# Link counts of a graph network layer: source nodes in rows and a fixed span of destination columns, and a fourth buffer of gathered rows

## Chip, cores and metric

The kernel runs on one core of one Trainium2 chip. The metric is device time in microseconds (us), the median of repeated runs. The core has a matrix engine (PE; PEld is its loading of weights), a vector engine (DVE), an activation engine (ACT), GpSimd (POOL), a queue engine (SP) and 16 DMA engines. On-chip memory is SBUF; matmul results land in PSUM, in banks of 512 f32 per partition.

## What is computed

There are 1250 nodes with 512 features (384 "vector", 128 "scalar") and 40000 edges, sorted by destination. The layer is PaiNN-like, followed by a residual and a layernorm:

```python
s_j = silu(x[src][:, 384:] @ W1 + b1) @ W3 + b3
edge_basis = rbf(edge_weight) * cutoff @ W2 + b2
s1, s2, s3 = thirds(s_j * edge_basis)
msg = concat(v_j * s1 + s3 * edge_attr, s2)          # first sums: over edges
x = x + segment_sum(msg, dst)
# node update: v@U, v@V, norm, an MLP, three factors -> row(x), a function of the node alone
x = x + segment_sum(row(x)[src], dst)                # second sums
out = layernorm(x0 + x)
```

The second sums need no edges once the number of links from each source node to each destination node is known: they are a matrix of link counts (dst x src) times the matrix of rows. The kernel makes these counts while it makes the first sums.

## The kernel before, in words

**Front.** Edges are cut into 79 chunks of 512 and laid out in rows. DVE tests that every edge lies in a window, and `by_tile` turns each field (source, destination less the chunk's first destination, weight, three attributes) with PE transposes into tiles of 128 edges. Then a table of node rows (640 wide) is made and written to DRAM.

**The loop over edge batches.** Four chunks make a group (20 groups, `g`). A step `t` of the loop takes four tiles of 128 edges, one of each chunk; a group has four steps, so there are 80 steps. In a step:

- POOL issues four indirect DMAs (`gather`, L649) that fetch 128 table rows each into `rows_t`, which has three buffers; the gather for step t+2 is issued in step t.
- PE makes the edge factors `eb` of the next step (`edge_factors`, L745). `eb` has one buffer, so this waits until DVE has finished the messages of the present step.
- DVE makes the messages (`messages`, L757 and L758) from `rows_t` and `eb`, then a one-hot of the source node's low part (`mark_sources`, L772), 256 wide.
- PE sums the messages of the step before (`add_messages`, L787 and L794) into `agg`, and counts its links (`count_links`, L811) into `adj`. Here the stationary operand is the hat function `pair` (32 columns for the 32 destination nodes of a chunk's window, one set for each of `PARTS` = 4 parts of the sources); the one-hot is the moving operand. Four tiles sit side by side in the array, each in 32 columns, so 16 matmuls of 256 columns a step.
- ACT makes the hats of the next group in `make_pair` (four L732, 128 wide, and one L737, 512 wide, a step).

1280 padded nodes don't fit into 4 x 256 sources; the fifth part is counted with a weight of 2^-11 on top of the first and split off later by DVE (`split_first`, L834 and L836).

**Closing a group.** After the group's last step, ACT copies `agg` and three quarters of `adj` out of PSUM (`close_group`, L821, L825, L826), DVE does `split_first`, and `hand_over` sends the rows that belong to a neighbouring block of nodes to `beside_s` and `beside_l` by DMAs on SP.

**A block of 128 nodes** (10 blocks, one for each two groups) is updated in ten steps that are spread through the loop: `make_sel` (DVE, then an ACT copy, L869) builds the selection of rows, `sum_block` (PE, L878) brings the first sums into node order, `take_block` adds them, `turn_nodes`, `times_u`, `u_times`, `times_v`, `lengths`, `hidden`, `factors`, `end_row` are small PE and ACT work through one PSUM buffer `work`, and `scale_row` (DVE, L1006 and L1012) needs the factor `s1` that ACT copies in L1000. `count_block` (L905, with an ACT copy L914) brings the counts of the block into node order: 30 matmuls for each block, in three of its steps.

**The second sums** (`add_out`, L1080) are 300 matmuls of 512 columns with `counts` as weights; most of them are spread over the last ten steps, after the last gather.

What sets the order: the program is recorded by hand. In each step the queues are filled in this order: gather, messages, mark_sources, the list `first`, add_messages and count_links of the step before, the list `early` (close_group, make_pair, block updates), edge_factors of the next step, the list `late`, the list `dve`. Every engine works through its own queue in that order.

```python
at(early, last_step[g] + 1, close_group, g)
at(early, t, make_pair, g + 1, i)
begin = max(last_step[last_source(b)] + 1, begin + 5)
at(dve, begin, make_sel, b)
at(late, begin + 4, count_block, b, BANK // P)
at(early, begin + 8, factors, b)
at(dve, begin + 8, scale_row, b)
```

The sine's arguments `turn` lie in the memory of `counts` until the first counts are written; most of their products are made on ACT in the first steps (`start_sine`, L671), 20 instructions.

Of the kernel before, what the change touches and what calls it, by code (L numbers as in the profile page):

```python
# [38 lines left out]
PARTS = 4  # L39
FIFTH = 2.0**-11  # L40
# [17 lines left out]
def gnn_resnorm(  # L58
# [121 lines left out]
    diff = const.tile([P, P], I32)  # L180
# [16 lines left out]
    sh.diff, sh.ident, sh.lane, sh.part, sh.half_n = diff, ident, lane, part, half_n  # L197
# [13 lines left out]
    nc.vector.tensor_scalar(share, part[:NCP, :], float(per_chunk), None, op0=ALU.mult)  # L211
# [4 lines left out]
    for values, bound, op in (  # L216
        (local_r, 0.0, ALU.is_lt),
        (away_r, float(-MARGIN), ALU.is_lt),
        (away_r, float(per_chunk + MARGIN - 1), ALU.is_gt),
    ):  # L220
        nc.vector.scalar_tensor_tensor(off, values, bound, off, op0=op, op1=ALU.max)
# [13 lines left out]
    sh.local = fields.tile([P, NGR, TPC * CPG], F32, name="local")  # L235
    sh.weight = fields.tile([P, NGR, TPC * CPG], F32, name="weight")
# [7 lines left out]
    with tc.tile_pool(name="ps_front", bufs=3, space=PSUM) as ps_front:  # L244
# [18 lines left out]
        for k in range(3):  # L263
            by_tile(att_r, k, 3, sh.attr[:, :, :, k])

# [213 lines left out]
def windowed(tc, sh):  # L479
# [18 lines left out]
    assert NP <= (PARTS + 1) * LOW and P == 2 * GSPAN and MARGIN <= GSPAN // CPG  # L498
# [43 lines left out]
    counts = keep.tile([P, NB, NB, P], F16, name="counts")  # L542
# [9 lines left out]
    with tc.tile_pool(name="msg", bufs=4) as pool, tc.tile_pool(  # L552
# [11 lines left out]
        turn = counts.rearrange("s b a n -> s (b a n)").bitcast(F32)[:, : NGR * N_RBF * EPG]  # L564
        turn = turn.rearrange("p (g n t) -> p g n t", n=N_RBF, t=EPG)
# [9 lines left out]
        column = pool.tile([P, NE], F32, name="column", bufs=1)  # L575
        fifth_e = pool.tile([P, NE], F32, name="fifth_e", bufs=1)
# [15 lines left out]
        def split_sources(half):  # L592
            if half == 0:
                nc.vector.tensor_scalar(fifth_e, src_f, PARTS * LOW - 0.5, None, op0=ALU.is_gt)
                nc.vector.scalar_tensor_tensor(
                    column, fifth_e, -float(PARTS * LOW), src_f, op0=ALU.mult, op1=ALU.add
                )
                nc.vector.tensor_scalar(
                    part, column, 1.0 / LOW, -0.5 + 0.5 / LOW, op0=ALU.mult, op1=ALU.add
# [5 lines left out]
                column[:, :, None].to_broadcast([P, NE, 2]), op0=ALU.mult, op1=ALU.add,  # L605
            )
            nc.vector.scalar_tensor_tensor(
                column, part, -float(WIN), sh.local.rearrange("p g t -> p (g t)"),
                op0=ALU.mult, op1=ALU.subtract,
            )  # L610
            nc.vector.tensor_scalar(fifth_e, fifth_e, 1.0 - FIFTH, None, op0=ALU.mult)
            nc.vector.scalar_tensor_tensor(
                column, column, 4.0, fifth_e, op0=ALU.mult, op1=ALU.add
# [4 lines left out]
        place = pool.tile([P, NB, 3, 2], F16, name="place", bufs=1)  # L618
        beside_s = pool.tile([P, 2, width], F32, name="beside_s", bufs=1)
        beside_l = pool.tile([P, 2, NP], F16, name="beside_l", bufs=1)  # L620
        nc.gpsimd.memset(beside_s, 0.0)
        nc.gpsimd.memset(beside_l, 0.0)
        def find_places():
            nc.vector.memset(place, -1.0)
            for b in range(NB):
                def put(rows, slot, g):
                    nc.vector.tensor_scalar(
                        place[rows, b, slot, :], sh.node[rows, g : g + 1].to_broadcast([rows.stop - rows.start, 2]),
                        float(-b * P), None, op0=ALU.add,
# [12 lines left out]
        aggs, adjs, sums, links, ebs, pairs, both_of = {}, {}, {}, {}, {}, {}, {}  # L642

        def gather(t):
            g, i = batches[t]
            rows_t = pool.tile([P, CPG, V + 2 * C], F32, name="rows_t", bufs=3)
# [13 lines left out]
        def start_turns(g, n):  # L660
# [4 lines left out]
                turn[:, g : g + n], share[:, :, None, :].to_broadcast(shape),  # L665
                sh.half_n[:, None, :, None].to_broadcast(shape),
            )

        def start_sine(g, k):

# [130 lines left out]
        def count_links(t):  # L801
            g, i = batches[t]
            if i == 0:
                adjs[g] = ps_sum.tile([P, PARTS * LOW], F32, name="adj")
# [768 lines left out]
```

## Time and profile before

| what | value |
|---|---|
| median of 14 runs | 612.78 us (610.52 to 618.65) |
| the profiled execution's own time | 612.09 us |
| its span | 610.3 us |
| mean granted clock of PE in the span | 0.908 |
| PE busy | 510.5 us, 84% |
| DVE busy | 443.8 us, 73% |
| POOL busy | 341.9 us, 56% |
| ACT busy | 302.2 us, 50% |
| first gather starts, last gather ends | 72.55 us, 493.56 us |

Reading it: busy shares are averages over stages with different limits. The front runs to about 72 us, the loop over gathered edges from there to about 500 us, the second sums and the layernorm to the end. Times in a view count from the start of the span. "Idle before, releaser" is how long the engine sat idle before an instruction and what ended that. The granted clock is a share of full speed. Matmul durations overlap, so for PE the chain of waits, or starts, tell more than the mean of one.

### The profile page before, as it was taken

Reading aid. Unit: us, or ns where it says so; the run is one execution under the profiler, and the core shown is the slowest. Engines: PE = TensorE matmul, PEld = TensorE weight load, DVE = VectorE, ACT = ScalarE, POOL = GpSimd, SP = SyncE. Lnnn points to the kernel's source line nnn. Section 1 sums busy time; section 2 is a strip of 40 time slices with the busy share of each in tenths; the row PEclk is TensorE's granted clock in tenths of the full one; section 3 lists DMA queues with packets and bytes.
Section 4 is the critical chain, followed back from the end, with each engine's and each line's share of the span. In section 5 each row is a group of like instructions: output and inputs, shape, how many; then the busy total and the mean of one; then the engine's idle time right before and its main releaser. Section 6 shows DMA issues by size and latency. Waiting matters only on the chain.

```text
span 610.3 us, 13655 instructions
## 1 busy us (share of the span) xinstructions
PE 510.5 (84%) x5626; PEld 280.4 (46%) x5626; DVE 443.8 (73%) x606; ACT 302.2 (50%) x717; POOL 341.9 (56%) x343
## 2 busy tenths in 40 slices
PE   1578547676999998998999998998888999999993
PEld 1322223233455455555554564564554645555441
DVE  4334069899789889999988898899989863020583
ACT  1210547255367468575684585675774632323200
POOL 2200177677777777777877777777777720044000
PEclk9965568799789889999998898899999899999997
DMA  8112288788978988888889888888788730701021
GB/s 242 49 64 86 91 253 259 224 246 250 286 241 252 288 253 257 267 254 271 249 252 283 253 259 266 256 257 264 229 269 262 241 106 18 261 27 72 35 86 53
DMA packets 37229, 124.12 MB, mean 203 GB/s; under 512 B 6738, under 2 KB 8104, under 8 KB 37158
## 3 DMA queue, kind: packets, MB, share of 16 engines
q0 software_dynamic: 25008, 102.42, 55.3%
q1 hardware_dynamic: 8230, 13.00, 6.1%
q10 hardware_dynamic: 3920, 7.74, 3.7%
q8 instruction: 46, 0.75, 0.5%
q14 instruction: 25, 0.20, 0.1%
HBM read 112.02 MB, written 8.46 MB: 197 GB/s over the span
## 4 chain that ended last, share of the span: by engine, by line
PE 50%; DMA 12%; DVE 11%; POOL 10%; issue 9%; ACT 8%; SPq 1%; DVEq 0%; POOLq 0%; ACTq 0%
POOL rows_t L649 10%; DMA rows_t<-table,src_i 9%; PE agg L787 7%; PE work L878 5%; PE eb L745 5%; PE agg L794 5%; PE adj L1080 4%; PE eb L1080 4%; DVE msg L758 3%; PE work L905 3%; PE adj L811 3%; ACT pair L732 2%; DVE msg L757 2%; PE agg L1080 2%; PE work L970 2%
## 5 line engine op out<-in xcount | busy, mean ns | idle before, releaser
L649 POOL DMA_INDIRECT rows_t<-table,src_i x313 | 320.7, 1025 | 150.1 <-issue 81.3
L758 DVE TENSOR_TENSOR msg<-rows_t,eb 128x1536 f32<-128x1536 f32 (+1 forms) x81 | 137.0, 1692 | 0.0
L757 DVE TENSOR_TENSOR msg<-rows_t,eb 128x1024 f32<-128x1024 f32 (+1 forms) x81 | 95.6, 1180 | 48.6 <-PE eb L745 23.4
L745 PE MATMUL eb<-w_sb,basis_t 21*128 21x384 f32 x626 | 78.5, 551 | 43.5 <-DVE msg L758 42.7
L732 ACT ACTIVATE pair<-number,column 128x128 f16<-128x128 f16 x320 | 102.0, 394 | 0.0
L787 PE MATMUL agg<-msg,hot 128*32 128x512 f32 x626 | 93.8, 656 | 0.0
L794 PEld LDWEIGHTS agg<-msg,spread 128*32 128x32 f32 x1878 | 58.9, 116 | 55.8 <-issue 55.5
L794 PE MATMUL agg<-msg,spread 128*32 128x128 f32 x1878 | 71.5, 282 | 0.0
L745 PEld LDWEIGHTS eb<-w_sb,basis_t 21*128 21x128 f32 x626 | 27.7, 189 | 62.3 <-issue 49.2
L811 PE MATMUL adj<-one,pair 128*32 128x256 f16 x1252 | 51.5, 276 | 4.0 <-DVE link L836 4.0
L772 DVE TENSOR_TENSOR one<-number,low 128x1024 f16<-128x1024 f16 (+1 forms) x81 | 53.8, 665 | 0.0
L737 ACT ACTIVATE pair<-pair 128x512 f16<-128x512 f16 x80 | 50.4, 630 | 2.5
L1080 PEld LDWEIGHTS <-counts 128*128 128x128 f16 x300 | 29.2, 98 | 33.0 <-issue 1.4
L1072 POOL TENSOR_TENSOR msg<-msg,rows_t 128x512 f32<-128x512 f32 (+1 forms) x10 | 13.0, 1328 | 52.4 <-PE work L990 41.9
L811 PEld LDWEIGHTS <-pair 128*32 128x32 f16 x1252 | 36.1, 98 | 5.7 <-issue 4.5
L720 DVE TENSOR_TENSOR spread<-hot,attr 128x768 f32<-128x768 f32 x40 | 38.0, 951 | 0.0
L905 PE MATMUL work<-sel_s,link 128*128 128x128 f16 x200 | 21.8, 230 | 12.1 <-ACT vu L939 11.4
L914 ACT ACTIVATE counts<-work 128x512 f16<-128x512 f32 (+1 forms) x30 | 15.8, 526 | 31.5 <-PE work L905 31.5
L1080 PE MATMUL eb<-store,counts 128*128 128x512 bf16 x120 | 28.5, 379 | 0.0
L703 ACT COPY basis_t<-work 128x512 f32<-128x512 f32 x20 | 11.7, 585 | 33.7 <-PE work L698 33.7
L905 PEld LDWEIGHTS <-link 128*128 128x128 f16 x200 | 16.2, 102 | 26.3 <-issue 25.3
L1027 ACT CAST store<-x 128x512 bf16<-128x512 f32 x10 | 6.2, 617 | 44.0 <-DVE x L1026 44.0
(177 smaller groups left out, 665.2 us busy)
## 6 DMA issues: line engine op xcount, KB each, us to landing
rows_t<-table,src_i POOLq DMA_INDIRECT x313
table<-msg SPq DMA_DIRECT2D x10, 320.0 KB
resid<-x SPq DMA_DIRECT2D x10, 256.0 KB
msg<-resid ACTq DMA_DIRECT2D x2, 1280.0 KB
out_dram<-msg SPq DMA_DIRECT2D x9, 256.0 KB
store<-in_x_dram ACTq DMA_DIRECT2D x2, 1024.0 KB
beside_l<-link SPq DMA_DIRECT2D x18, 80.0 KB
rows_t<-in_x_dram ACTq DMA_DIRECT2D x1, 1280.0 KB
```

The source lines that it names most:

```text
L649: nc.gpsimd.indirect_dma_start(out=rows_t[:n, j, :], out_offset=None, in_=sh.table1, in_offset=bass.IndirectOffsetOnAxis(ap=sh.src_i[:n, g ...
L732: nc.scalar.activation(pair[:, e, :], number[:, : PARTS * WIN], AF.Abs, scale=4.0, bias=column[:, g * EPG + e : g * EPG + e + 1],)
L737: nc.scalar.activation(quarter, quarter, AF.Relu, scale=-1.0, bias=1.0)
L745: nc.tensor.matmul(eb[:, j, :V], turned[g][rows, i, :], sh.w2_sb[rows, :], start=True, stop=True,)
L757: nc.vector.tensor_mul(msg[:m, js, V:], rows_t[:m, js, V:], eb[:m, js, C:V])
L758: nc.vector.tensor_mul(msg[:m, js, :V].rearrange("p t (k c) -> p t k c", k=3), rows_t[:m, js, :V].rearrange("p t (k c) -> p t k c", k=3), ...
L772: nc.vector.tensor_tensor(one[:m, js, :].rearrange("p t (l h) -> p t l h", h=2), number[:m, :].rearrange("p (l h) -> p l h", h=2)[:, None] ...
L787: nc.tensor.matmul(agg[j * WIN : (j + 1) * WIN, :], hots[g][:m, i * CPG + j, :], msg[:m, j, :width], start=(i == 0), stop=False, skip_grou ...
L794: nc.tensor.matmul(agg[j * WIN : (j + 1) * WIN, c * C : (c + 1) * C], spread[g][:m, i * CPG + j, c, :], msg[:m, j, width:], start=False, s ...
L811: nc.tensor.matmul(adj[j * WIN : (j + 1) * WIN, k * LOW : (k + 1) * LOW], pairs[g][:m, i * CPG + j, k * WIN : (k + 1) * WIN], one[:m, j, : ...
L905: nc.tensor.matmul(out[:, a * P : (a + 1) * P], t[:rows, (first + a) * P : (first + a + 1) * P], sels[b][1][:rows, n, :], start=(k == 0), ...
L1080: nc.tensor.matmul(acc, counts[:, b, a, :], table2(a, k), start=(a == 0 and k == 0), stop=(a == NB - 1 and k == 2),)
```

## The change

The counts are now summed with the *source* nodes in the rows. `count_links` takes the one-hot as stationary operand, in two halves of 128 source nodes, and the hats as moving operand: for each tile and each half one matmul, 128 rows out, 5 x 48 = 240 columns. The 48 columns are a fixed span of destination nodes, the same for all edges of a chunk (16 of the chunk's own and a margin of 16 on each side), and no longer the 32 from the chunk's first destination; `PARTS` is 5, so the weight of 2^-11 and `split_first` go. A group covers 96 columns, of which 32 overlap with the group before: `close_group` copies the new 64 for all parts into `counts` (ACT, 640 elements), and `add_counts` adds the overlapping 32 to what stands there (DVE, 320 elements). `counts` is then in the order in which `add_out` uses it: `count_block`, the `link` tiles, `beside_l` with its DMAs and the small selection are gone; the big selection is made by DVE directly. `make_pair` is 240 wide (and 960 for its second pass). A field `away` is turned in the front in addition. `turn` gets a small tile of its own for two groups and its products are made in `make_turns` on DVE; `start_turns` and `start_sine` go. `rows_t` gets a fourth buffer; the gather for step t+2 is still issued in step t. `beside_s` with two slots becomes `flank` with one.

```diff
-PARTS = 4
-FIFTH = 2.0**-11
+PARTS = 5
+SPAN = GSPAN // CPG + 2 * MARGIN
+REACH = GSPAN - GSPAN // CPG + SPAN
...
+        by_tile(away_r, 0, 1, sh.away)
...
-    counts = keep.tile([P, NB, NB, P], F16, name="counts")
+    counts = keep.tile([P, NB, NGR * GSPAN + REACH], F16, name="counts")
+    by_group = counts.rearrange("s (p h) n -> s h p n", h=2)
...
-            rows_t = pool.tile([P, CPG, V + 2 * C], F32, name="rows_t", bufs=3)
+            rows_t = pool.tile([P, CPG, V + 2 * C], F32, name="rows_t", bufs=4)
...
-        def start_turns(g, n):
+        def make_turns(g, n):
...
-                turn[:, g : g + n], share[:, :, None, :].to_broadcast(shape),
+                turn[:, :n], share[:, :, None, :].to_broadcast(shape),
...
-                pairs[g] = pool.tile([P, EPG, PARTS * WIN], F16, name="pair", bufs=2)
+                pairs[g] = pool.tile([P, EPG, PARTS * SPAN], F16, name="pair", bufs=2)
...
-                    pair[:, e, :], number[:, : PARTS * WIN], AF.Abs, scale=4.0,
+                    pair[:, e, :], number[:, : PARTS * SPAN], AF.Abs,
...
-                adjs[g] = ps_sum.tile([P, PARTS * LOW], F32, name="adj")
+                adjs[g] = ps_sum.tile([P, 2, BANK], F32, name="adj")
...
-            for k in range(PARTS):
+            for h in range(2):
+                to = adj[:, h, : PARTS * REACH].rearrange("s (p n) -> s p n", n=REACH)
...
+                    at = j * (GSPAN // CPG)
...
-                        adj[j * WIN : (j + 1) * WIN, k * LOW : (k + 1) * LOW],
-                        pairs[g][:m, i * CPG + j, k * WIN : (k + 1) * WIN], one[:m, j, :],
+                        to[:, :, at : at + SPAN], one[:m, j, h * P : (h + 1) * P],
+                        pairs[g][:m, i * CPG + j, :].rearrange("e (p n) -> e p n", n=SPAN),
...
-            nc.scalar.copy(link[:rows, LOW:BANK], adj[:rows, LOW:BANK])
-            nc.scalar.copy(link[:rows, BANK : PARTS * LOW], adj[:rows, BANK:])
...
-        def split_first(g):
...
+            adj = adjs[g][:, :, : PARTS * REACH].rearrange("s h (p n) -> s h p n", n=REACH)
+            new, reach = REACH - GSPAN if g else 0, tiles(g, 0)[-1] * GSPAN // CPG + SPAN
+            nc.scalar.copy(
+                by_group[:, :, :, g * GSPAN + new : g * GSPAN + reach], adj[:, :, :, new:reach]
+            )
+
+        def add_counts(g):
+            adj = adjs.pop(g)[:, :, : PARTS * REACH].rearrange("s h (p n) -> s h p n", n=REACH)
+            if g:
+                to = by_group[:, :, :, g * GSPAN : (g + 1) * GSPAN - (2 * GSPAN - REACH)]
+                nc.vector.tensor_add(to, to, adj[:, :, :, : REACH - GSPAN])
...
-            nc.sync.dma_start(beside_s[rows, slot, :], sums[g][rows, :])
-            nc.sync.dma_start(beside_l[rows, slot, :], links[g][rows, :])
+            nc.sync.dma_start(flank[rows, :], sums[g][rows, :])
...
-            sel = pool.tile([P, 3, P], F32, name="sel", bufs=1)
-            nc.scalar.copy(sel, small)
-            sels[b] = sel, small
+            sels[b] = sel
...
-        def count_block(b, first):
...
-                        acc, counts[:, b, a, :], table2(a, k),
+                        acc, counts[:, a, MARGIN + b * P : MARGIN + (b + 1) * P], table2(a, k),
...
-        at(dve, 0, start_turns, 1, 2)
-        for k in range(N_RBF):
-            at(late, 1 + k * 4 // N_RBF, start_sine, 3, k)
...
-            at(dve, last_step[g] + 1, split_first, g)
+            at(dve, last_step[g] + 1, add_counts, g)
...
-            at(late, begin + 3, count_block, b, 0)
...
-            at(late, begin + 4, count_block, b, BANK // P)
...
-            at(late, begin + 5, count_block, b, 2 * BANK // P)
```

## The prediction

> **What bounds the kernel now.** I read the page's busy shares first, then the table of stretches by block of nodes, then the chain of waits for the tail, then the timeline of single steps.
>
> ```profile
> PE 510.5 (84%) x5626; PEld 280.4 (46%) x5626; DVE 443.8 (73%) x606; ACT 302.2 (50%) x717; POOL 341.9 (56%) x343
> L649 POOL DMA_INDIRECT rows_t<-table,src_i x313 | 320.7, 1025 | 150.1 <-issue 81.3
> ...
> 115.49 1.15 POOL L649 DMA_INDIRECT rows_t<-table,src_i  x1 [2.25 <-DVE msg L758]
> ```
>
> POOL's 56% hides a full queue. From 72.55 to 493.56 us it gathers, and each of 313 gathers costs its 1.025 us plus about 0.30 us of issue: 1.325 us, so 32 gathers (one block of nodes, eight steps) can't take less than 42.4 us. In all that time it waited only some 5 us for a buffer, 2.25 of them at 115.49.
>
> ```profile
> core 0: us, PE busy (x) PEld busy (x) DVE busy (x) ACT busy (x) POOL busy (x), PEclk, DMA share, GB/s
> 156.90:200.80 43.90, 40.52 (x535) 23.52 (x534) 38.37 (x44) 27.02 (x65) 33.85 (x34) 0.93 0.84 259
> 244.10:285.00 40.90, 37.59 (x535) 22.37 (x536) 39.48 (x46) 27.89 (x67) 31.46 (x32) 1.00 0.86 261
> 370.60:414.90 44.30, 40.90 (x535) 23.57 (x536) 39.56 (x46) 28.22 (x68) 33.88 (x34) 0.92 0.85 260
> ```
>
> These are three of the seven blocks between 156.9 and 456.9 (300.0 us, 42.86 us each). DVE works 39.5 us in the block of 40.9 us: there DVE is the bound, with 1.4 us of waits. In the blocks of about 44 us the granted clock is 0.92 to 0.93. So three limits lie within 3 us of each other: POOL 42.4, DVE 40.9 (with its waits), and PE when its clock drops.
>
> ```profile
> 384.00:388.00 4.00, 2.77 (x50) 1.85 (x43) 3.96 (x7) 3.36 (x9) 3.09 (x4) 1.00 0.81 247
> 388.00:392.00 4.00, 3.80 (x40) 2.23 (x43) 3.97 (x6) 2.54 (x7) 3.08 (x4) 0.57 0.78 240
> ...
> 388.20 0.27 PE L905 MATMUL work<-sel_s,link 128*128 128x128 f16 x2 [1.40 <-ACT vu L939]
> 389.25 1.94 PE L787 MATMUL agg<-msg,hot 128*32 128x512 f32 x8
> ```
>
> PE stood 1.40 us at the second `count_block` of the block, because `work` has one buffer and ACT's copy (L939) stands behind `make_pair`; then the clock was 0.57 and `add_messages` took twice its time. Five blocks have this; their step starts of L757 are 6.4 to 7.1 us apart, where undisturbed ones are 4.7.
>
> ```profile
> 409.21 0.25 ACT L1000 COPY s<-work 128x128 f32<-128x128 f32 x1
> 409.49 0.56 DVE L1006 TENSOR_TENSOR x<-vu,s 128x384 f32<-128x384 f32 x1 [0.57 <-ACT s L1000]
> ...
> 496.68 1.70 PE adj L811 x12
> 511.99 0.83 PE work L905 x12
> 516.33 0.83 PE work L905 x12
> 520.39 0.34 PE work L905 x6
> 538.05 0.69 PE work L905 x12
> ```
>
> The first pair shows DVE waiting on ACT once in every block. The others are pieces of the chain that ended last: after about 463 us it is nearly all PE, so there each PE instruction less is time less.
>
> **The change, part by part.** The sum is made against the profiled execution: 612.09 us, of which 610.3 are the span. It lies 0.7 us under the median of 612.78, well within the runs' spread.
>
> *Front, +0.7.* `by_tile(away)` puts four transposes behind the twelve of the attributes; four cost 0.74 us (L253, local_r). PE, the test, DVE's first work and the table's chain follow one another there, so I take it whole; ends 0 and +1.2 (with ACT's 0.43 copy). Shorter `split_sources` and one memset instead of two (L621 0.96, L622 2.24) lie beside the table's chain, which waits on PE and ACT: nothing.
>
> *Fourth buffer, -2.0.* The wait at 115.49 goes (2.25 less the usual 0.30). What is late next is DVE: the step that starts at 101.43 takes it 10.9 us (`find_places` 5.6) and now loses L834 and L836 (0.84), since `add_counts` does nothing for group 0; with those the 4.0 us that PE waited for L836 once go too. Ends -2.0 and 0. Later waits for a buffer are 0.05 to 0.3 us each: nothing.
>
> *PE in a step.* Now 16 matmuls in 0.44 us (chain, L811 at full clock). After: 8 of 240 columns. L905 starts 128 columns every 0.056 us, L1080 512 columns every 0.215, both with full 128x128 weights; between them 240 columns cost 0.10, so 0.82: +0.38 a step, 3.0 a block (ends 0.45 and 1.72 for the eight, by the two rows). Gone are 30 matmuls a block (0.78, 0.78 and 0.44 us) and the stall of 1.2 to 1.4: -3.3. PE's sum stays, but it is laid out evenly.
>
> *ACT in a step.* L732 (128 wide) follow each other by 0.295, L737 (512 wide) takes 0.63; slope 0.61 to 0.86 ns an element (the second from L821 against L1000). So 4 x 0.07 to 0.10 and 0.27 to 0.39: +0.55 to +0.77 a step. Gone are L914, L825, L826, L869 and L671; the new copy of 640 elements costs about 0.70 (L821's slope). ACT's total has room (28 of 42 us), its order has not: the root in `lengths` stands behind `make_pair`, `hidden` and `add_messages` behind it on PE, then ACT's two copies, `make_pair` again, and only then `s1`. That is +0.55 (first pass), +0.38 (longer counts), +0.55 (second pass), less 0.15 (copies): `s1` comes 1.3 us later, ends 0.8 and 2.1. DVE stands in `scale_row` for it; behind it are `make_sel` and the next messages, and PE's next `eb` waits for these.
>
> *DVE in a block.* Minus 0.83 twice (L834, L836); plus 0.49 twice (`add_counts`, 320 elements on L836's 0.42 for 256); plus 0.82 (L664's product, now every second group); plus 0.15 (f32 selection). Of the savings, those just before the wait for `s1` are lost in it.
>
> *A block's period.* 40.9 (undisturbed) - 0.4 + 0.82 + 0.15 + 1.3 + 0.3 (two steps where PE is now level with DVE) = 43.1. Half-clock spells at L905 go with their stall; those at `sum_block` (L878 4.46 against 2.77 us, about every second block, after a wait for DVE that stays) leave 0.2: 43.3 against 42.86, seven times: +3.1. Ends: POOL's floor of 42.4 gives -3.2; `s1` 2.1 late and spells in every block, 44.5, gives +11.
>
> [...]
>
> *Last block of the loop (456.9 to 501.3), -2.0.* Its stall and spell go (1.5); the mixed step, where 12 matmuls over tiles of 128 and 64 rows took 1.70, becomes six of 0.10 (-1.1); some 0.6 is given back as above. Ends -5 and +1.
>
> *Tail, -5.1.* Before 517.15 the L905 at 511.99 and 516.33 go, and ACT's copies in between shrink; PE is then ready for L1080 at about 514.1, when ACT's last copy lands: -3.05. Behind that PE is full, so L905's 0.34, 0.69, 0.69 and 0.34 are all time: -2.06. Ends -6.5 and -3.
>
> *Free.* [...] The DVE product may hold a gather up (the one beside L664 took 1.40 instead of 0.95): at most 4.5 us over ten blocks, covered by the 0.9 us a block between POOL's floor and 43.3, and paid if DVE were quicker.
>
> Sum: 0.7 - 2.0 + 3.1 - 2.0 - 5.1 = -5.3: 606.8 us.
>
> **The rivals.**
>
> *`s1` decides (slower).* ACT's longer passes make DVE wait in each block. For it: L1006 already waits for L1000 in most blocks. Against it: ACT idles a third of a block. It turns the sign when the block exceeds 44.05 us, which is `s1` 2.1 late; at 2.6 late, 44.6: +12.2 instead of +3.1, 615.9 us.
>
> *POOL becomes the clean bound (much faster).* With the stall gone PE keeps full clock, the fourth buffer takes up every unevenness, and a block costs 42.4: 606.8 - 6.3 = 600.5 us. For it: the three blocks at clock 1.00 need 40.9 to 42.2. Against: `s1`.
>
> *Full-width counting costs PE what L1080 costs.* If strided sums of 5 x 48 columns cost 0.215 each, a step gains 1.3 us of PE, a block 7 more: about 45.5, +18: 622 us. Nothing in the trace speaks for it but the missing row.
>
> *No gain in the tail.* If the last counts hold L1080 up by 3 us, the tail saves 2.1 and the time is about 610.
>
> **How the numbers follow.** Forecast as summed (604 to 609.5) 0.38; POOL's floor 0.22; nothing much (609.7 to 615.8) 0.20; `s1` 0.14; PE 0.06. Half a per cent, 3.1 us, is about what a measurement of this kernel can tell. Under 609.7: 0.38 + 0.22 = 0.60, less 0.02 for the forecast's upper edge, 0.58; over 615.8: `s1` and PE, 0.20; between: 0.20 + 0.02 = 0.22. The ends of all terms reach 595 and 622; 8 in 10 lie in 598.5 to 616; the likeliest case alone lies in 603 to 611.
>
> **What the profile after would show.** Eight matmuls of 240 columns a step in 0.8 us; no wait of 1.4 us and no drop of clock in the block's fifth step; DVE's wait for `s1` about 2.2 us a block; ACT's passes 0.36 and 0.9 us; POOL without the 2.25; L1080 starting about 6 us earlier than 517. Wrong if DVE's wait for `s1` is under 1 us or over 3, if the eight matmuls cost over 1.1 us, or if half-clock spells are as many as before.

## The result, and the profile after

The changed kernel takes 635.3 us (median, 631.3 to 637.8), the kernel before 613.0: a ratio of 1.036 (95% interval 1.033 to 1.039). It is slower by 22 us where 6 us less were forecast, and it lies far above the range. Lines of `kernel.py` have moved: the messages are L741 and L742 (before L757, L758), `count_links` L797 (L811), `edge_factors` L729 (L745), `sum_block` L852 (L878), the copy of `s1` L954 (L1000), `add_out` L1034 (L1080), the gather L643 (L649).

The page of after: busy shares, and the granted clock in 40 slices of the span (the second fence is before's row of the same view).

```profile
PE 528.1 (84%) x4704; PEld 288.2 (46%) x4704; DVE 442.5 (70%) x590; ACT 333.5 (53%) x638; POOL 343.4 (55%) x342
PEclk9965579889997987987987987987987999999998
```

```profile
PEclk9965568799789889999998898899999899999997
```

PE has 922 matmuls fewer and is busy 18 us longer. From the thirteenth slice to the thirty-first, that is from about 190 to 490 us, its clock falls to 0.7 in every third slice. The table of stretches shows the loop (columns: stretch, length, busy time of PE, weight loads, DVE, ACT and POOL, granted clock, share and rate of the DMAs):

```profile
core 0: us, PE busy (x) PEld busy (x) DVE busy (x) ACT busy (x) POOL busy (x), PEclk, DMA share, GB/s
244.00:292.00 48.00, 43.36 (x441) 24.58 (x441) 40.38 (x45) 31.67 (x60) 35.84 (x35) 0.89 0.81 249
387.00:435.00 48.00, 43.29 (x441) 24.64 (x440) 40.02 (x45) 31.67 (x60) 33.67 (x33) 0.89 0.76 229
```

A block of eight steps takes 47.65 us on average from step 21 to step 69, and 47.8 in each of the last three of these; before it took 42.65 between the same steps. No engine is full in it: PE works 43.3 us of 48, DVE 40, POOL 33.5. Cut at the starts of the messages of steps 0, 21, 69 and 79 and at the first matmul of the second sums, the spans compare so (us; the last column is an experiment told below):

| stretch | before | after | filler_long |
|---|---|---|---|
| front, to step 0 | 81.1 | 78.4 | 77.7 |
| steps 0 to 21 | 115.0 | 113.2 | 114.1 |
| steps 21 to 69, six blocks | 255.9 | 285.9 | 260.1 |
| steps 69 to 79 | 49.3 | 50.2 | 47.1 |
| step 79 to the first matmul of the second sums | 15.7 | 11.0 | 10.9 |
| from there to the end | 93.3 | 91.2 | 91.3 |
| span | 610.3 | 629.9 | 601.2 |

Up to step 21 the changed kernel is 4.5 us ahead, and it saves 6.8 us behind step 79. The six blocks between lose 30.0. This is one of them on PE (the timeline of after: start, us, operation, count, and in brackets how long PE had been idle and what ended it):

```profile
317.92 0.93 PE L729 MATMUL eb<-w_sb,basis_t 21*128 21x384 f32 x8 [1.34 <-DVE msg L742]
319.13 0.65 PE L682 MATMUL work<-ident,basis 128*128 128x128 f32 x4 [0.28 <-ACT vv L916]
319.71 1.86 PE L771 MATMUL agg<-msg,hot 128*32 128x512 f32 x8
321.32 1.53 PE L778 MATMUL agg<-msg,spread 128*32 128x128 f32 x24
326.47 1.07 PE L771 MATMUL agg<-msg,hot 128*32 128x512 f32 x8
...
337.18 1.66 PE L729 MATMUL eb<-w_sb,basis_t 21*128 21x384 f32 x8 [2.07 <-DVE msg L742]
338.77 3.78 PE L852 MATMUL work<-sums,sel 128*128 128x512 f32 x4
```

The same eight `add_messages` take 1.86 us at 319.71 and 1.07 at 326.47. PE idles 1.34 and 0.28 us, works at half clock for 3.4 us, idles 2.07 us some steps later, and works at half clock for 6.8. On DVE (timeline of after) the first idle place begins with the product (L658, 0.82 us), the second with the wait for `s1`; each spell comes back as a wait for `eb`:

```profile
312.77 0.82 DVE L658 TENSOR_TENSOR turn<-weight,half_n 128x640 f32<-128x640 f32 x1
325.97 1.22 DVE L741 TENSOR_TENSOR msg<-rows_t,eb 128x1024 f32<-128x1024 f32 x1 [2.12 <-PE eb L729]
332.62 0.56 DVE L960 TENSOR_TENSOR x<-vu,s 128x384 f32<-128x384 f32 x1 [1.90 <-ACT s L954]
338.90 1.22 DVE L741 TENSOR_TENSOR msg<-rows_t,eb 128x1024 f32<-128x1024 f32 x1 [1.27 <-PE eb L729]
347.57 1.22 DVE L741 TENSOR_TENSOR msg<-rows_t,eb 128x1024 f32<-128x1024 f32 x1 [1.96 <-PE eb L729]
```

Where do the spells begin and end? In steps of 0.25 us, the granted clock of after falls at 289.1, 319.9, 336.9, 367.6, 384.7 us: 9 and 5 times 3.413 us apart, in turn. The shorter of the spells, from 319.85 to 323.26, lasts 3.41 us itself, and from the fall at 108.23 to that at 480.28 it is 109 times 3.413. So I cut the loop into stretches of 3.413 us that end where a spell begins (the table of stretches again):

```profile
313.02:316.43 3.41, 3.41 (x50) 2.30 (x46) 3.34 (x5) 1.83 (x6) 2.55 (x3) 1.00 0.90 260
316.43:319.85 3.42, 1.79 (x18) 0.90 (x20) 3.42 (x5) 2.64 (x7) 2.75 (x3) 1.00 0.78 262
319.85:323.26 3.41, 3.41 (x35) 1.69 (x31) 3.41 (x4) 3.36 (x7) 2.50 (x4) 0.50 0.83 226
323.26:326.67 3.41, 3.41 (x29) 2.55 (x31) 1.29 (x2) 2.59 (x3) 2.80 (x3) 1.00 0.78 246
333.50:336.91 3.41, 1.42 (x8) 0.98 (x6) 3.41 (x4) 3.35 (x8) 1.44 (x2) 1.00 0.85 236
336.91:340.33 3.42, 3.15 (x10) 1.38 (x11) 2.15 (x4) 1.71 (x3) 2.42 (x3) 0.50 0.45 137
340.33:343.74 3.41, 3.41 (x5) 1.01 (x3) 3.25 (x4) 0.00 (x0) 2.80 (x3) 0.50 0.84 237
343.74:347.15 3.41, 3.41 (x49) 1.87 (x48) 1.50 (x3) 0.62 (x1) 2.50 (x4) 1.00 0.87 236
```

All 28 changes of the clock of after between 120 and 530 us lie at edges of this grid. PE was busy for 0.52 and 0.42 of the stretches ahead of the spells. In after, of 98 stretches at full clock between 120 and 530 us, the 13 in which PE was busy for less than 0.55 are all followed by half clock, and of the 85 at 0.63 and above one is (0.69). In after, half clock ended only behind a stretch that was full, and the second spell, which began with 0.3 us of idle time, lasted twice as long; in three_buffers_2 and more_work it also ended behind 0.95 and 0.96, so that this is no exact rule.

The trace of before has a grid of the same step: its clock falls at 327.1, 344.2, 371.5 and 388.6 us, 5, 8 and 5 times 3.413 us apart. Nine of its ten spells between 120 and 530 us follow stretches with shares of 0.39 to 0.61, though between 0.52 and 0.61 eight were followed by half clock and seven were not. The tenth, at 501.22, follows a stretch in which the profile has PE busy throughout (1.00, in 19 matmuls). So the share goes with the spells, but it is not what the clock goes by.

### The profile page after: what moved, and what is told of

Same layout as the page of the kernel before. It is cut to its first block, busy times and chain, and to the rows that moved or that the text cites. A ratio compares the mean times of both kernels' runs of the same rounds, so it can differ in the third digit from the quotient of the medians.

```text
span 629.9 us, 11657 instructions
## 1 busy us (share of the span) xinstructions
PE 528.1 (84%) x4704; PEld 288.2 (46%) x4704; DVE 442.5 (70%) x590; ACT 333.5 (53%) x638; POOL 343.4 (55%) x342
## 4 chain that ended last, share of the span: by engine, by line
PE 32%; DVE 20%; POOL 18%; DMA 13%; issue 12%; ACT 3%; DVEq 0%; SPq 0%; POOLq 0%; ACTq 0%
POOL rows_t L643 18%; DMA rows_t<-table,src_i 11%; DVE msg L742 7%; PE work L852 5%; DVE msg L741 4%; PE adj L1034 4%; PE eb L1034 4%; PE eb L729 3%; PE agg L771 2%; DVE one L756 2%; PE agg L1034 2%; PE adj L797 2%; PE agg L778 1%; PE eb L471 1%; PE eb L470 1%
## 5 line engine op out<-in xcount | busy, mean ns | idle before, releaser
L643 POOL DMA_INDIRECT rows_t<-table,src_i x313 | 324.9, 1038 | 171.2 <-issue 81.1
L741 DVE TENSOR_TENSOR msg<-rows_t,eb 128x1024 f32<-128x1024 f32 (+1 forms) x81 | 95.6, 1180 | 64.0 <-PE eb L729 44.5
L742 DVE TENSOR_TENSOR msg<-rows_t,eb 128x1536 f32<-128x1536 f32 (+1 forms) x81 | 137.0, 1692 | 0.0
L729 PE MATMUL eb<-w_sb,basis_t 21*128 21x384 f32 x626 | 84.0, 584 | 59.6 <-DVE msg L742 58.9
L716 ACT ACTIVATE pair<-number,away 128x240 f16<-128x240 f16 x320 | 131.7, 484 | 0.0
L721 ACT ACTIVATE pair<-pair 128x960 f16<-128x960 f16 x80 | 80.2, 1003 | 2.5
L797 PE MATMUL adj<-pair,one 128*128 128x240 f16 (+1 forms) x626 | 80.2, 271 | 0.0
L729 PEld LDWEIGHTS eb<-w_sb,basis_t 21*128 21x128 f32 x626 | 30.2, 199 | 77.8 <-issue 59.5
L797 PEld LDWEIGHTS <-one 128*128 128x128 f16 (+1 forms) x626 | 55.5, 99 | 20.6 <-issue 15.3
L1034 PEld LDWEIGHTS <-counts 128*128 128x128 f16 x300 | 29.4, 98 | 33.9 <-issue 1.4
L852 PE MATMUL work<-sums,sel 128*128 128x512 f32 (+1 forms) x40 | 32.3, 954 | 0.0
L771 PEld LDWEIGHTS agg<-msg,hot 128*32 128x32 f32 x626 | 12.9, 110 | 40.1 <-issue 32.0
L960 DVE TENSOR_TENSOR x<-vu,s 128x384 f32<-128x384 f32 x10 | 5.8, 583 | 36.0 <-ACT s L954 36.0
L808 ACT COPY sums<-agg 128x512 f32<-128x512 f32 (+1 forms) x20 | 11.7, 586 | 32.8 <-PE agg L778 32.8
```

The source lines that it names most:

```text
L643: nc.gpsimd.indirect_dma_start(out=rows_t[:n, j, :], out_offset=None, in_=sh.table1, in_offset=bass.IndirectOffsetOnAxis(ap=sh.src_i[:n, g ...
L716: nc.scalar.activation(pair[:, e, :], number[:, : PARTS * SPAN], AF.Abs, bias=column[:, g * EPG + e : g * EPG + e + 1],)
L721: nc.scalar.activation(quarter, quarter, AF.Relu, scale=-1.0, bias=1.0)
L729: nc.tensor.matmul(eb[:, j, :V], turned[g][rows, i, :], sh.w2_sb[rows, :], start=True, stop=True,)
L741: nc.vector.tensor_mul(msg[:m, js, V:], rows_t[:m, js, V:], eb[:m, js, C:V])
L742: nc.vector.tensor_mul(msg[:m, js, :V].rearrange("p t (k c) -> p t k c", k=3), rows_t[:m, js, :V].rearrange("p t (k c) -> p t k c", k=3), ...
```

## The experiments

Three theories stood against each other. 1, the clock: each block has two stretches in which PE has too little to do, and the spells behind them cost the time. 2, ACT: its longer passes of `make_pair` make `s1` late, and the clock is incidental. 3, the product on DVE starts it. None of these kernels leaves out or changes anything of the result; the fillers and more_work do needless work in addition.

**Needless work for PE** (filler, filler_3, filler_long). Nothing is moved or removed. Small f16 matmuls into 32 columns of `adj` that nothing reads are put ahead of `edge_factors` in the two places where PE idles.

```diff
+        def keep_busy(t, n):
+            g, i = batches[t - 1]
+            for k in range(n):
+                nc.tensor.matmul(
+                    adjs[g][:, k % 2, PARTS * REACH :], number[:, :P], number[:, P : P + 32],
+                    start=False, stop=False, skip_group_check=True,
+                )
...
+            if g > 0 and group_rows(g) == P and g % 2 == 0 and i == 2:
+                at(early, t, keep_busy, t, 24)          # filler_long: 46
+            if g > 0 and group_rows(g) == P and g % 2 == 1 and i == 1:
+                at(early, t, keep_busy, t, 36)          # filler_long: 70
```

Expected of the first form:

> The changed kernel with nothing taken away: 24 small matmuls (128 rows, 32 columns, f16) into unused columns of adj ahead of edge_factors in the third step of an even group, and 36 in the second step of an odd group, the two places where PE idles 1.34 and 2.07 us. They are work that no result needs. Theory 1, the clock gate: the two stretches are busy for more than 0.6 of 3.41 us, no spell of half clock follows, and the block falls by the 5.3 us that the spells cost, to 42.5: about 601 us, although every wait for s1 and for the product stays. Theory 2 and theory 3, in which ACT's passes or DVE's product hold the loop and the clock is incidental: nothing goes or some us are added, 635 to 640.

> The changed kernel with 24 and 36 small needless matmuls in the two places of each block where PE idles 1.34 and 2.07 us, once more, to see whether the engines still stand for instructions as in the runs so far (the kernel before at about 850 us instead of 613). Where they don't: by theory 1, the clock gate, both stretches of 3.41 us are busy for more than 0.6, no half clock follows, the block falls from 47.7 to 42.5 us and the time to about 601 us, although no wait was removed. By theories 2 and 3, in which the clock is incidental, 635 to 640.

Measured in filler_3: 625.6 us, one run, beside 609.8 of the kernel before. The matmuls were shorter than the gaps, and the same place went both ways (timelines of filler_3, a block apart):

```profile
271.92 0.76 PE L808 MATMUL adj<-number 128*128 128x32 f16 x24
273.42 0.93 PE L729 MATMUL eb<-w_sb,basis_t 21*128 21x384 f32 x8 [0.75 <-DVE msg L742]
275.21 1.78 PE L771 MATMUL agg<-msg,hot 128*32 128x512 f32 x8
...
319.69 0.76 PE L808 MATMUL adj<-number 128*128 128x32 f16 x24
321.19 0.93 PE L729 MATMUL eb<-w_sb,basis_t 21*128 21x384 f32 x8 [0.75 <-DVE msg L742]
322.98 1.06 PE L771 MATMUL agg<-msg,hot 128*32 128x512 f32 x8
```

With 0.75 us left idle, half clock followed at 275 and not at 323; both stretches were busy for 0.70 by the profile. So here too the profile's busy time is not exactly what the clock goes by. The expectation of 601 us by theory 1 was missed. The longer form:

> The changed kernel with about twice the needless matmuls, 46 and 70. In filler_3 24 of them took 0.71 us and 36 took 1.06, PE still idled 0.75 and 1.18 us in the two places, and half clock followed in some blocks and not in others; blocks without the first spell took 45 us instead of 47.7. 46 and 70 take 1.36 and 2.07 us and fill both gaps. Theory 1, the clock gate: no block has either spell, each waits still for s1 and for the product, and takes 42.5 us: the loop's 6.4 blocks save 33 us, 601 us. If the gate doesn't count such small matmuls as work: as filler_3 or a little slower, 625 to 632. Theories 2 and 3, the clock is incidental: 635 to 645.

Measured: 605.5 us, a ratio to before of 0.987 (0.984 to 0.991), 30 us less than the changed kernel. In the loop (table of stretches, then the timelines of PE and DVE of filler_long):

```profile
250.00:300.00 50.00, 47.62 (x651) 30.22 (x644) 46.41 (x52) 36.53 (x70) 38.73 (x38) 1.00 0.81 251
...
322.62 1.91 PE L808 MATMUL adj<-number 128*128 128x32 f16 x70
324.86 0.93 PE L729 MATMUL eb<-w_sb,basis_t 21*128 21x384 f32 x8 [0.33 <-DVE msg L742]
...
320.30 0.56 DVE L968 TENSOR_TENSOR x<-vu,s 128x384 f32<-128x384 f32 x1 [2.25 <-ACT s L962]
```

From 139 us to the end of the loop the clock is 1.00, a block takes 43.35 us instead of 47.65, and DVE still waits 1.6 to 2.25 us for `s1` in each block. Theories 2 and 3 expected 635 or more. The clock is the cause of the loss, and the waits are not, except that they made the gaps.

**`make_pair` at the end of the step** (late_pair_3).

```diff
-                at(early, t, make_pair, g + 1, i)
...
+        for t, (g, i) in enumerate(batches):
+            if g + 1 < NGR:
+                at(late, t, make_pair, g + 1, i)
```

> The changed kernel with make_pair at the end of each step's list late; expected as in label late_pair. Theory 1, the clock gate: the wait for s1 (1.9 us a block) goes, PE's idle 2.07 us behind it and the spell of 6.8 us of half clock go with it, the block falls from 47.7 to about 43 us, the time to about 605. Theory 2, ACT's passes by themselves: only the 1.9 us a block, 623. Theory 3, the product starts the pattern: 630 or more.

Measured: 605.0 us, 0.982 (0.976 to 0.989). The wait for `s1` is gone in the loop, a block takes 43.05, and 6 spells are left between 100 and 510 us, where after has 15. The 605 of theory 1 came out, not the 623 of theory 2: the wait of 1.9 us was worth more than twice itself. One thing theory 1 had not said: the first place still has its gap, 1.26 us at 220.62 and 1.34 at 270.48, 312.57, 355.34, 400.01 and 441.46, and half clock followed at 355.34 alone. The gap now falls elsewhere in the grid; the windows that hold it were busy for 0.55 at 355.34, and for 0.61 at 270.48 and 400.01.

**The product in the `sum_block` step** (moved_product_3). `make_turns` is cut in two, and its product is recorded six steps earlier.

```diff
-        def make_turns(g, n):
+        def multiply_turns(g, n):
...
+        def make_turns(g, n):
             args = turn[:, :n].rearrange("p g n t -> p (g n t)")
...
                     at(dve, t, make_hot, g + 1)
+                    if g % 2 and g + 2 < NGR:
+                        at(dve, t, multiply_turns, g + 2, min(2, NGR - 2 - g))
```

> The changed kernel with the product of make_turns (0.82 us of DVE) recorded in the sum_block step; expected as in label moved_product. Theory 1, the clock gate: the idle 1.34 us of PE shrinks to about 0.5, the spell of 3.4 us behind it goes, 45.0 us a block, 618 us. Theory 2: 630. Theory 3, the product alone starts the pattern: 602.

Measured: 612.6 us, 0.998 (0.995 to 1.001). The first spell is gone from every block, as theory 1 has it, and beyond that the second comes in only four of seven, though PE's gap of 2.07 us is there in all seven (stretches of moved_product_3, one for each block, then its timeline of PE in two blocks):

```profile
236.20:282.00 45.80, 41.13 (x483) 24.75 (x482) 40.30 (x45) 34.32 (x67) 35.75 (x34) 1.00 0.80 248
282.00:325.00 43.00, 38.79 (x403) 22.09 (x406) 39.26 (x44) 28.95 (x55) 33.25 (x33) 0.92 0.83 257
325.00:371.00 46.00, 41.36 (x484) 24.96 (x484) 40.37 (x46) 34.52 (x68) 35.53 (x35) 1.00 0.82 252
371.00:414.00 43.00, 38.77 (x402) 21.96 (x405) 39.00 (x43) 28.90 (x55) 32.88 (x33) 0.92 0.82 255
...
331.75 0.93 PE L731 MATMUL eb<-w_sb,basis_t 21*128 21x384 f32 x8 [2.07 <-DVE msg L744]
332.61 1.99 PE L854 MATMUL work<-sums,sel 128*128 128x512 f32 x4
...
374.77 1.66 PE L731 MATMUL eb<-w_sb,basis_t 21*128 21x384 f32 x8 [2.07 <-DVE msg L744]
376.37 3.78 PE L854 MATMUL work<-sums,sel 128*128 128x512 f32 x4
```

(The cuts lie in the middle of a block, so a spell that delays one block stands in the next stretch.) From step 21 on, five blocks alternate between 45.8 and 43.0 us, cut at the messages, and the sixth takes 44.3. The same wait before the same matmuls cost a spell at 374.77 and none at 331.75, so a gap by itself doesn't set the clock. The one ahead of 374.77 lies in the window from 371.20 but for 0.16 us, and PE was busy for 0.38 of that; the one ahead of 331.75 is cut by the edge at 330.24, and PE was busy for 0.56 of the window behind the edge. Moving 0.82 us of DVE saved 23 us. Theory 1 had asked for 618, theory 2 for 630, theory 3 for 602; theory 1 is nearest, but none gives 612.6, because each took a gap to have the same effect in every block.

**Both moves** (late_product_3), and **both with three buffers** (late_product_3buf; `bufs=3` in the three places of `rows_t`).

> Both moves together; expected as in label late_product. Theory 1, the clock gate: neither of the two stretches is left, a block takes what DVE and PE need at full clock, or POOL's 42.4 us if that is more: 598 to 602. Theory 2 (ACT alone): no better than make_pair's move alone. Theory 3 (product alone): no better than the product's move alone.

> make_pair late and the product in the sum_block step, with three buffers of gathered rows: what the fourth buffer is worth where POOL is the bound (a block of 42.6 us in late_product_3 stands against POOL's 42.4). If the fourth buffer takes up the unevenness of the steps: 0.3 to 1 us a block without it, 607 to 612. If it is worth nothing: 604.8 as late_product_3, within 2.

Measured: 604.8 us, 0.985 (0.978 to 0.992), and with three buffers 603.6, 0.979 (0.973 to 0.986). The second is the lowest median of all, though the intervals overlap. The moves don't add up; the lines suggest the next bound, but no run shows it by itself. The groups of late_product_3 (last columns: idle time ahead, and what ended it):

```profile
L643 POOL DMA_INDIRECT rows_t<-table,src_i x313 | 322.5, 1030 | 149.3 <-issue 84.4 <-DMA table<-msg 54.2 <-DMA rows_t<-table,src_i 4.9
L743 DVE TENSOR_TENSOR msg<-rows_t,eb 128x1024 f32<-128x1024 f32 (+1 forms) x81 | 95.7, 1182 | 47.5 <-DMA rows_t<-table,src_i 27.8 <-PE eb L731 14.3 <-PE agg L780 2.3
```

POOL's idle time is the start (54.2) and its own issue (84.4); it waits for no buffer to speak of, and DVE waits for gathered rows (27.8 us, 11.4 of them for the first; in after 18.7, 11.8 of them for the first). A block takes 42.6 us, beside the 42.4 that the prediction gave POOL; five spells are left in the loop behind 120 us. Theory 1 expected 598 to 602; of what is missing, 4.5 us lie in the front, which took 82.9 us to step 0 in this run, with the code of after (78.4).

**Three buffers in the changed kernel** (three_buffers_2).

> The changed kernel with three buffers of gathered rows instead of four: what the fourth buffer is worth by itself. Theory 1: the locked rhythm of 47.7 us a block is set by PE and DVE, POOL waits there 30 us for buffers anyway, so the time stays at 635 within 3. The prediction's step gave the fourth buffer 2.0 us: then 637. Theory 5, that the fourth buffer started the pattern: 625 or less.

Measured: 635.6 us, 1.033 (1.026 to 1.040): no difference. Steps 0 to 21 took 115.0 us, 1.8 more than in after; this can't be put down to the buffer, because late_product_3buf with three took 112.8 there and late_product_3 with four 114.8. The blocks behind them took 47.8 again, but for the first (46.2).

**More work for DVE** (more_work). A quarter of `make_spread` is done twice in each block.

```diff
+                    if g % 2 == 0:
+                        at(dve, t, more_work, g)
```

> The changed kernel with a needless repetition of a quarter of make_spread on DVE (0.55 us) in the first step of each even group. In the trace after, blocks take 47.65 to 47.8 us, and 14 windows of the clock are 47.79. If the block is locked to the windows (each block meets the same window in the same place, whatever the work), 0.55 us more of DVE change nothing: 47.8 us a block, 635 us. If the times simply add: 48.3 us a block, 639. If it moves the gaps in the windows so that a spell is missed: below 630.

Measured: 634.8 us, 1.032 (1.024 to 1.039). Half a microsecond more in each of nine blocks cost nothing. Blocks were no longer equal: 44.0, 46.7, 48.5, 48.1, 46.8, 48.5 us, a mean of 47.1 from step 21 to 69; in some the first spell was missed. That the times add is refuted; that every block sits on 14 windows (47.79 us), as in after and three_buffers_2, holds only while the gaps meet the windows in the same places.

**The kernel before with `make_pair` late** (before_late_pair; the same edit in the kernel before).

> The kernel before the change, with make_pair at the end of each step's list late: is the gain of that move the change's own remedy, or would it have helped anyway? Theory 1: before, ACT's copies behind make_pair cause the wait for s1 (0.6 to 1.1 us a block) and the stall of 1.2 to 1.4 us at the second count_block, and five to seven spells of half clock; they go, a block falls from 42.65 to POOL's 42.4 at best, 2 to 4 us in all: 609 to 611. If the move is worth the same 30 us in both kernels: 583.

Measured: 611.6 us, 0.995 (0.990 to 1.000). So the move mends something that the change broke. The changed kernel with the same order had 0.982 on another chip, so with both in that order the change is worth about 1.3%, some 8 us: an estimate from the two ratios, with some 0.8% either way by their intervals.

**On two other chips** (late_pair, moved_product, filler, three_buffers; late_pair_2, moved_product_2, filler_2, late_product). These are the same kernels as above. On the first chip:

> The changed kernel, with make_pair recorded at the end of each step's list late instead of in early, so that no make_pair stands ahead of s1's copy on ACT. Theory 1, the clock gate: the trace after shows half clock behind every stretch of 3.41 us in which PE was busy for less than some 0.55; the wait for s1 (1.9 us a block) makes one of these stretches (PE idle 2.07 us before eb of the sum_block step). Without the wait that spell of 6.8 us goes as well: the block falls from 47.7 to about 43 us, and over the 6.4 blocks that show the pattern the time falls by about 30 us, to 605. Theory 2, ACT's longer passes cost by themselves and the clock is incidental: only the wait goes, 1.9 us a block, 12 us, 623. Theory 3, the product in make_turns starts the pattern: the block stays above 47, 630 or more.

> The changed kernel, with the product of make_turns (L658, 0.82 us) recorded six steps earlier, at the end of DVE's work on the basis in the sum_block step, where DVE waits for PE anyway. Theory 1, the clock gate: PE's idle 1.34 us in the third step of the even group shrinks to about 0.5, the spell of 3.4 us behind it goes, with the product itself 2.7 us a block: 45.0 us a block, 618 us. Theory 2, ACT's passes start everything: only the 0.8 us move, and as DVE's spare time takes them 5 us at most go: 630. Theory 3, the product alone starts the pattern: both spells go, 42.5 a block, 602.

> The changed kernel with three buffers of gathered rows instead of four: the counting alone. All theories but one put the loss into the counting: the time stays at 635, within 4 us (up to 3 us more, as the first 22 steps lose part of the 5 us by which they were ahead). Theory 5, the fourth buffer lets POOL's gathers fall differently beside DVE's work and so starts the pattern: the time falls by 10 us or more.

On the second:

> The changed kernel with make_pair at the end of each step's list late, on another chip: on the first one all engines stood for instructions (label late_pair: PE waited for 'issue' tens of us in the loop and the kernel before took 849 us), which hides the theories' differences. Expected as there. Theory 1, the clock gate: the wait for s1 (1.9 us a block) goes, PE's idle 2.07 us behind it and the spell of 6.8 us of half clock go with it, the block falls from 47.7 to about 43 us, the time to about 605. Theory 2, ACT's passes by themselves: only the 1.9 us a block, 623. Theory 3, the product starts the pattern: 630 or more.

> The changed kernel with 24 and 36 small needless matmuls in the two places of each block where PE idles 1.34 and 2.07 us, on another chip. Theory 1, the clock gate: both stretches of 3.41 us are then busy for more than 0.6, no half clock follows, and the block falls by the 5.3 us of the spells: about 601 us, although no wait was removed. Theories 2 and 3, the clock is incidental: 635 to 640.

> The changed kernel with the product of make_turns (0.82 us of DVE) recorded in the sum_block step, on another chip. Theory 1, the clock gate: the idle 1.34 us of PE shrinks to about 0.5, the spell of 3.4 us behind it goes, 45.0 us a block, 618 us. Theory 2: 630. Theory 3, the product alone starts the pattern: 602.

> Both moves together: make_pair in the list late, the product in the sum_block step. Theory 1, the clock gate: neither of the two stretches is left, a block takes what DVE and PE need at full clock, or POOL's 42.4 us if that is more: 598 to 602. Theory 2 (ACT alone): no better than make_pair's move alone, 623. Theory 3 (product alone): no better than the product's move alone.

There the kernel before took 849 and 847 us, and these eight kernels 759 to 778. Weight loads stood longer without a wait that the profile shows ("issue"), and DVE waited 69.6 us in three_buffers for signals whose source the profile doesn't show, 0 in three_buffers_2. Such waits hide the differences between the theories; that they were waits for instructions, as two of the expectations have it, was not shown. From the waits of the weight loads, three_buffers on the first of these chips, and three_buffers_2, the same kernel, on another:

```profile
PEld agg L778 <- issue: 94.4, 201, 1.3
```

```profile
PEld agg L778 <- issue: 54.5, 164, 0.8
```

The changed kernel's code, but for the buffer, took 772.8 us there against 849.2: 9% faster than before, where it is 3% slower elsewhere. They are left out of the comparison of theories. Why both kernels were slower there stays open, and so does whether it is the smaller number of PE instructions that pays there.

## Why the prediction was wrong

*Step that failed: a block's period.* The forecast was 43.3 us; the trace has 47.65. The other terms of the sum were right together: without its 0.2 for spells it is 43.1, and with the clock held up by needless work a block takes 43.35. The term that was mis-sized is the spells, "Half-clock spells at L905 go with their stall; those at `sum_block` [...] leave 0.2". The spells went at L905 and came back in two other places, for 4.3 us a block. Six blocks of that are 25.8 us, and steps 69 to 79, which have a spell too, 3.1 more: the whole distance of 28.7 us between the spans of after and filler_long, but for 0.2 us in the rest. The forecast's 0.2 has no working: one spell of 1.7 us (4.46 against 2.77) in every second block would be 0.85. And its own sign of being wrong was there: between 100 and 510 us after has 15 spells, before 12.

*How the row was misread.* At 388.20 the trace of before showed a gap of 1.40 us and half clock behind it. I took the gap at that line for the cause. But of the eight such stalls of 1.2 to 1.5 us at L905 in before, three (260.06, 300.91, 430.96) were not followed by half clock. What the spells go with in these traces, if not exactly (13 of 13 windows under 0.55 in after, eight of 15 from 0.52 to 0.61 in before), is how much of a window of 3.41 us PE is busy, whatever the lines; before, the window was this (table of stretches of before):

```profile
385.16:388.57 3.41, 1.98 (x21) 1.27 (x21) 3.38 (x6) 2.96 (x9) 2.71 (x3) 1.00 0.79 239
388.57:391.99 3.42, 3.42 (x37) 1.85 (x38) 3.39 (x5) 2.39 (x6) 2.59 (x3) 0.50 0.79 260
```

The share is 0.58, where it went both ways. The change gave DVE 0.82 us more in one step and a longer wait for `s1` in another (in the loop 12.4 us in seven blocks, before 2.5 in five), and two windows fell to 0.52 and 0.42 in every block. Moving the product and moving `make_pair` show these two parts. That the change also took PE work away (30 matmuls a block) may have added to it; no run shows that. The forecast counted the L905 matmuls as pure gain: "PE's sum stays, but it is laid out evenly." It stayed, but PE's idle time came together in two places.

*The rivals.* "`s1` decides" had the sign and named the place, but not the mechanism: it gave 615.9 us for an `s1` that is 2.6 us late, and with the clock held up the wait is up to 2.25 us, some 1.75 more than before, and the time 605.5. The prediction's reading that DVE waited for `s1` in every block of before was too wide: it did in five of eight, for 0.46 to 0.57 us. POOL as the clean bound is close to what late_product_3 shows (42.6 us a block). PE at L1080's rate is out: eight L797 follow each other into the next operation in 0.83 us (from 301.94 to 302.77), 0.82 forecast. No rival was "the spells move".

*The other terms*, by the table of the result:

- Front, +0.7: after's is 2.7 shorter. It can't be read, because the front of the same code took 77.7 to 82.9 us in these runs (last section).
- Fourth buffer, -2.0: not shown. Steps 0 to 21 took 1.8 less in after than in three_buffers_2, but 2.0 more in late_product_3 than in late_product_3buf, and nothing is left of it in either median.
- ACT, +0.55 to +0.77 a step: the four L716 take 1.65 instead of 1.28 us, L721 1.00 instead of 0.63, so +0.74.
- The wait for `s1`, about 2.2: 1.3 to 1.9 in after, 1.6 to 2.25 in filler_long.
- DVE: L821 0.48 (0.49 forecast), L658 0.82.
- Last block, -2.0 (steps 69 to 79): +0.9 in after, -2.2 in filler_long, so the term was right and the spell was missing. The mixed step's six counts took 1.03 us, not 0.6, against 1.70.
- Tail: from the last messages of the loop to the first matmul of the second sums, -4.7 against -3.05, of which some 1.7 are a spell that before had at L878 (3.67 us for four matmuls, after 1.98). Behind that, -2.1 against -2.06.

The timeline of after for the tail, where PE has no gap ahead of the second sums:

```profile
527.58 1.98 PE L852 MATMUL work<-sums,sel 128*128 128x512 f32 x4
...
538.00 0.84 PE L889 MATMUL work<-u_sb,x_t 128*128 128x128 f32 x6
538.67 0.81 PE L1034 MATMUL agg<-store,counts 128*128 128x512 bf16 x3
```

## What to carry to other kernels

When a trace shows spells of half clock, measure how far apart they begin (in these traces multiples of 3.413 us), cut it into windows of that length that end where a spell begins, and read PE's busy share in each; a change that makes PE wait a microsecond longer has to be checked against the windows that are low (here, under some 0.75: 13 of 13 under 0.55 in after were followed by half clock, and at 0.74 to 0.76 some were and some were not, in late_pair_3 those at 240.41 and 284.78). A sum of durations can be right to some 0.3 us a block and the time still be off by 28 us, if the change lets the loop meet the same windows in every round, as the six blocks of after did. The remedy is to move what makes PE wait, or, as a probe, to give it needless work in the gap: that told the clock from the waits without removing a wait (clock 1.00 and 43.35 us a block in filler_long, with 1.6 to 2.25 us of waiting for `s1` left).

## What the runs showed of the hardware that I had not expected

- The granted clock changed only on a fixed grid of 3.413 us: all 28 changes of after between 120 and 530 us and all 20 of before. A window at full clock in which PE was busy for less than 0.55 was followed by half clock in each of 13 cases of after; from 0.52 to 0.61 it went both ways in before. Where the edge lies, and in what unit, stays open. With 24 or 36 matmuls of 32 columns in the window the profile of filler_3 said 0.65 to 0.73, and half clock followed in 10 of 13 cases. Without any such work it followed windows at 0.74 to 0.76 in late_pair_3, late_product_3 and late_product_3buf (eight cases), and one at 1.00 in before.
- The same gap of 2.07 us of idle PE was followed by half clock in four of seven blocks of moved_product_3: so at 374.77, where its window was busy for 0.38, and not at 331.75, where an edge of the grid cut it and the window behind was busy for 0.56.
- The loop fell into step with this grid in after and again in three_buffers_2, at 47.8 us a block, 14 windows; half a microsecond more of DVE work in a block didn't show in the time (more_work, 634.8 us against 635.3).
- The front, whose code is nearly the same in after and its variants, took 77.7 to 78.5 us where the grid lay 2.3 to 2.6 us behind the start of the span, 80.9 to 81.1 at 2.8 to 3.4 and at 0.6, and 82.8 to 82.9 at 1.5 to 1.7 (nine traces). So up to 5 us of the time of one run go with where the grid lies when it starts; no run moved the grid alone.
